# A graph attention kernel: the queries of the last node blocks made after the walk's first gathers are issued, instead of in the projection

## The chip, the cores and the metric

The kernel runs on one core of one Trainium2 chip. The metric is device microseconds of one execution. A profile is one execution that the hardware profiler recorded; its span reaches from the first to the last instruction.

## The reference

A graph layer on 12,500 nodes with 256 features and 200,000 edges that are sorted by their target `dst`. `D` is 32, there are 8 heads.

```python
h = relu(layernorm(x))
q = (h @ Wq + bq);  k = (h @ Wk + bk);  v = (h @ Wv + bv)      # heads of 32
logits = einsum('ehd,ehd->eh', q[dst], k[src]) / sqrt(32)
attn = softmax of logits over the edges with the same dst
agg = segment_sum(attn[:, :, None] * v[src], dst)
y = h + gelu(agg + h @ Wskip + bskip)
out = x + layernorm(y) * gamma + beta
```

## The kernel before

**Projection.** `project()` (from L154) goes over 98 blocks of 128 nodes, in 23 groups of 1, 2, 4, then sixteen times 5, then 4, 4, 2 and 1 blocks (`sizes`, `starts`). For each block TensorE (PE) turns `h` with the help of an identity matrix (L141), ScalarE (ACT) copies the turned `h` from PSUM to `hT` (L143), PE multiplies it with `w_kv` into `ps_kv` (L258) and with `w_q` into `ps_q` (L264). VectorE (DVE) adds the biases (L261 for k and v, L268 for q). q is stored as two parts: ACT rounds it to fp32r (L269, the high part), GpSimd (POOL) takes the difference (L270, the low part). For each group the sync engine's queue (SP) stores `h` to `h_tab`, k and v to `kv_tab` (L273) and the two parts of q to `q_pc` (L275). Wq and bq are multiplied by 1/sqrt(32) once, at the start.

**Plan.** In the same stretch `make_plan()` turns the lists of edges into tables for the walk: `idx` (which rows to gather), `e_tab`, `pen_tab`, `d0_row`, `slot_row` and a flag. Its `behind` puts some of its instructions behind given blocks of the projection, in the fixed order of an engine: a share of the list `biased` (one entry for each q addition, L268) or of `products` (one entry for each product with `w_kv` or `w_q`). A flag read by each engine then decides between `walk_streams` and another way that isn't taken here (L350).

**Walk.** `walk_streams()` goes over the edges in 66 steps. The edges are cut into 8 streams; a step takes up to 3 tiles (`j`) of 128 edges from each. For one tile, 8 indirect DMAs on POOL (`gather`, L1058) fetch the rows of k and v by `src`, 128 rows of 2 KB each. There are 6 tiles for this, 3 for each of two steps. SP loads `et` (`prefetch`, L1030), `pen` (`penalties`, L1036) and the q rows of the nodes in the step's windows, `qw` (`windows`, 8 loads at L1050 from `q_pc`). PE and ACT make a matrix `to_e` from `et` (`hot_e`, L1075 and L1077), PE spreads q over the edges with it (`spread`, L1098), DVE multiplies with k (`times`, L1107) and sums over each head (`total`, L1114). After maxima over the segments (L1133 to L1136) and the exponential (L1140), DVE weighs v (`weigh`, L1162, with L1167 or L1169 for the denominators), and PE sums per node (L1192). SP stores the sums to `table`.

Every instruction of the walk goes through `keep`, which orders it behind the one before it on the same engine; so each engine's order is the order in which the program writes the calls.

At the start of the walk the program writes: `prefetch`, `penalties` and `windows` of step 0, `prefetch` and `penalties` of step 1, then the gathers of steps 0 and 1 (48 in all, with `windows(1)` and `prefetch(2)` between them on SP), then `hot_e` of step 0, `spread`, `hot_e` of step 1, and the first multiplications. The next gathers come from `gather_next`, two at a time: the first two of them fill tile 1 of step 0 anew and stand behind `weigh(0, 1)`.

**Final pairs.** From the step `FIN_FIRST` = 10 on, pairs of blocks whose sums are complete are finished within the walk. Class `Pair` takes its tiles from the pool `fin`: `sums`, `x_f`, `h`, `o` with two buffers each, and `hT` with one. It turns `h` in a bank of `hot_ps` (transposes at L858, copy at L861), multiplies with `w_s` (L878), and so on. `hot_ps` and `qe_ps` have two PSUM buffers each. Until step 10 the tiles of `fin` lie unused.

Of the kernel before, what the change touches and what calls it, by code (L numbers as in the profile page):

```python
# [28 lines left out]
F32 = mybir.dt.float32  # L29
F32R = mybir.dt.float32r  # L30
# [4 lines left out]
OP = mybir.AluOpType  # L35
# [4 lines left out]
PSUM = bass.MemoryType.PSUM  # L40
DRAM = bass.MemoryType.DRAM

P = 128
# [28 lines left out]
def gnn_kernel(ctx: ExitStack, tc: tile.TileContext, x, src, dst, Wq, bq, Wk, bk, Wv, bv,  # L72
               Wskip, bskip, gamma, beta, out):
    nc = tc.nc
    N, HID = x.shape
    E = src.shape[0]
    D = HID // HEADS
    KC = HID // P
    SUMS = HEADS * (D + 1)
    KV = 2 * HID  # L80
    NBLK = N // P + 1
# [6 lines left out]
    h_tab = dram.tile([NP, HID], F32, name="h_tab")  # L88
# [56 lines left out]
    def norm_stats(pool, t, mean, rstd):  # L145
# [8 lines left out]
        nc.scalar.activation(rstd, mv[:, :, 1], AF.Sqrt, bias=eps)  # L154
        nc.vector.reciprocal(rstd, rstd)

    def project():


# [3 lines left out]
            tc.add_manual_dep(ins.ins, other.ins.name, mybir.DependencyInfo(  # L163
                mybir.DependencyClass.NoSync, mybir.DependencyReason.DATA), reason="kept order")

        sizes = [1] * NBLK
        if NBLK >= 14:
            mid = NBLK - 14
            sizes = [1, 2, 4] + [5] * (mid // 5) + [mid % 5] * (mid % 5 > 0) + [4, 2, 1]
        with tc.tile_pool(name="proj_c", bufs=1) as cpool, \  # L170
                tc.tile_pool(name="proj", bufs=2) as pool, \
                tc.tile_pool(name="proj_ps", bufs=2, space=PSUM) as psum:
# [11 lines left out]
                    nc.sync.dma_start(xt[:N % P, 0, :], x[b0 * P:, :])  # L184
                return xt

            starts = [sum(sizes[:i]) for i in range(len(sizes))]
            x_in = [load(0, sizes[0])]
            w_kv = cpool.tile([P, KC, 2 * HID], F32, name="w_kv")
            b_kv = cpool.tile([P, 2 * HID], F32, name="b_kv")  # L190
# [6 lines left out]
                rows(t, a)  # L197
            weights(w_q, Wq)
            rows(b_q, bq)
            qscale = 1.0 / math.sqrt(D)  # L200

            def prepare(g):

# [30 lines left out]
            for g, (b0, n) in enumerate(zip(starts, sizes)):  # L234

                if g > 1 and g + 1 < len(sizes):
                    ready[g + 1] = prepare(g + 1)
                if g == (4 if len(sizes) < 16 else 13):
                    make_near(tc, near, near_n, lambda ins: behind(ins, last))
                if g == (3 if len(sizes) < 16 else 12):  # L240
                    for ins in [rows(gam, gamma)] + \
                            [weights(w_s, Wskip)]:
                        behind(ins, products[-1])
                    pieces(b_s3, bskip, 1.0)
                    pieces(b_o3, beta, 1.0)
                    zero = cpool.tile([WN, HID], F32, name="zero")
                    nc.vector.memset(zero, 0.0)
                    for k in range(2):
                        behind(nc.scalar.dma_start(q_pc[NP:, k * HID:(k + 1) * HID], zero),
                               products[-1])  # L250
                h = ready.pop(g)
                kvo = pool.tile([P, 5, KV], F32, name="kvo")[:, :n, :]
                qp = pool.tile([P, 5, 2, HID], F32R, name="qp")[:, :n]
                for b in range(n):
                    hT, turned = transposed(pool, psum, h[:, b, :])
                    ps_kv = psum.tile([P, 2 * HID], F32, name="ps_kv", bufs=3)
                    for c in range(KC):
                        ins = nc.tensor.matmul(ps_kv, hT[:, c, :], w_kv[:, c, :], start=c == 0,  # L258
                                               stop=c == KC - 1)
                    products.append(ins)  # L260
                    nc.vector.tensor_tensor(kvo[:, b, :], ps_kv, b_kv, op=OP.add)  # L261
                    ps_q = psum.tile([P, HID], F32, name="ps_q", bufs=1)
                    for c in range(KC):
                        ins = nc.tensor.matmul(ps_q, hT[:, c, :], w_q[:, c, :], start=c == 0,  # L264
                                               stop=c == KC - 1)
                    products.append(ins)
                    q = qp[:, b, 1, :].bitcast(F32)
                    biased.append(nc.vector.tensor_tensor(q, ps_q, b_q, op=OP.add))  # L268
                    nc.scalar.copy(qp[:, b, 0, :], q)  # L269
                    nc.gpsimd.tensor_tensor(qp[:, b, 1, :], q, qp[:, b, 0, :].bitcast(F32),  # L270
                                            op=OP.subtract)
                for tab, t in ((h_tab, h), (kv_tab, kvo)):
                    nc.sync.dma_start(tab[b0 * P:(b0 + n) * P, :]  # L273
                                      .rearrange("(p b) d -> p b d", p=P), t)
                nc.sync.dma_start(q_pc[b0 * P:(b0 + n) * P, :]  # L275
                                  .rearrange("(p b) d -> p (b d)", p=P),
                                  qp.rearrange("p b k d -> p (b k d)").bitcast(F32))
                if g < 2:
                    ready[g + 1] = prepare(g + 1)
        return products, biased  # L280

    def queries(q_tab):

        with tc.tile_pool(name="qry", bufs=2) as pool:
            for b in range(NBLK):
                t = pool.tile([P, 2, HID], F32, name="q_in")
                nc.sync.dma_start(t, q_pc[b * P:(b + 1) * P, :]
                                  .rearrange("p (k d) -> p k d", k=2))
                q = pool.tile([P, HID], F32, name="q")
                nc.vector.tensor_add(q, t[:, 0, :], t[:, 1, :])  # L290
                nc.sync.dma_start(q_tab[b * P:(b + 1) * P, :], q)
# [58 lines left out]
    with tc.If(fits > 0) as branch:  # L350
        table = dram.tile([S, NT, KV], F32, name="table")
        walk_streams(tc, N, HID, NST, KL, many, ident, idx, d0_row, slot_row, near, near_n, e_tab, pen_tab,
                     h_tab, kv_tab, q_pc, table, x, out, w_s, one_row, b_s3, b_o3, gam, eps)
    with branch.Else():
        gtab = dram.tile([NP + P, SUMS + HEADS], F32, name="gtab")
        q_tab = dram.tile([NP, HID], F32, name="q_tab")
        queries(q_tab)
        walk_partitions(tc, src, dst, N, NP, HID, ident, flag, q_tab, kv_tab, gtab, dram)
        with tc.tile_pool(name="gfin", bufs=2) as pool, \
# [63 lines left out]
def make_plan(tc, pool, ep, psum, src, dst, N, LEN, NST, SLACK, NT, dram, ident, flag, idx, d0_row,  # L423
# [4 lines left out]
    nc = tc.nc  # L428
# [3 lines left out]

    def behind(ins, share):

        tc.add_manual_dep(ins.ins, biased[len(biased) * share // 100].ins.name,
                          mybir.DependencyInfo(mybir.DependencyClass.NoSync,
                                               mybir.DependencyReason.DATA), reason="kept order")

# [327 lines left out]


def walk_streams(tc, N, HID, NST, KL, many, ident, idx, d0_row, slot_row, near, near_n, e_tab, pen_tab, h_tab,
                 kv_tab, q_pc, table, x, out, w_s, one_row, b_s3, b_o3, gam, eps):

# [4 lines left out]
    nc = tc.nc  # L775
# [200 lines left out]
    with ExitStack() as es:  # L976
# [247 lines left out]
        extra = [m for m in rest if m >= SURE]  # L1224
        rest = [m for m in rest if m < SURE]

        prefetch(0)
        penalties(0)
        windows(0)
        prefetch(1)  # L1230
        penalties(1)
        for c in range(2):
            for j in range(tiles_of(c)):
                gather(c, j)
            if c == 0:
                windows(1)
                prefetch(2)
        for i in range(QT):
            hot_e(0, i)
        for half in range(2):  # L1240
# [611 lines left out]
```

## Time and profile before

| what | value |
|---|---|
| median of 3 runs | 2433.07 us (2431.04 to 2437.38) |
| profiled execution | 2429.78 us, its span 2428.1 us |
| granted TensorE clock, mean | 0.743 |

By stages of the profile, busy us of each engine, granted clock and GB/s moved:

| stage, us from the span's start | length | PE | DVE | ACT | POOL | clock | GB/s |
|---|---|---|---|---|---|---|---|
| projection and plan, up to block 81 (0 to 287.2) | 287.2 | 253.2 | 226.4 | 111.8 | 124.3 | 0.99 | 264 |
| projection, last 16 blocks, and the branch (287.2 to 338.4) | 51.2 | 44.6 | 29.6 | 12.5 | 19.6 | 1.00 | 255 |
| walk, first 48 gathers (338.4 to 398.8) | 60.4 | 25.0 | 33.4 | 12.6 | 45.8 | 0.50 | 255 |
| walk, the other gathers (398.8 to 2336.0) | 1937.2 | 1313.7 | 1663.4 | 896.1 | 1471.5 | 0.71 | 277 |
| end (2336.0 to 2428.1) | 92.1 | 60.8 | 44.1 | 28.4 | 3.3 | 0.67 | 89 |

A line of the timeline gives start, length, engine, line and operation, with the written tile to the left of the arrow and the read ones to its right; in brackets stands how long the engine had been idle and what released it. `SPq` is the sync engine's DMA queue; its lengths are those of the issue, not of the transfer. A line of the chain of waits gives start, length and what the chain ran through.

### The profile page before, as it was taken

Reading aid. Unit: us, or ns where it says so; the run is one execution under the profiler, and the core shown is the slowest. Engines: PE = TensorE matmul, PEld = TensorE weight load, DVE = VectorE, ACT = ScalarE, POOL = GpSimd, SP = SyncE. Lnnn points to the kernel's source line nnn. Section 1 sums busy time; section 2 is a strip of 40 time slices with the busy share of each in tenths; the row PEclk is TensorE's granted clock in tenths of the full one; section 3 lists DMA queues with packets and bytes.
Section 4 is the critical chain, followed back from the end, with each engine's and each line's share of the span. In section 5 each row is a group of like instructions: output and inputs, shape, how many; then the busy total and the mean of one; then the engine's idle time right before and its main releaser. Section 6 shows DMA issues by size and latency. Waiting matters only on the chain.

```text
span 2428.1 us, 29469 instructions
## 1 busy us (share of the span) xinstructions
PE 1697.2 (70%) x7824; PEld 904.4 (37%) x7824; DVE 1996.9 (82%) x2461; ACT 1061.4 (44%) x2323; POOL 1664.4 (69%) x1751
## 2 busy tenths in 40 slices
PE   6999974555556766667667777676777677667685
PEld 3555532222233333333333333333333333334343
DVE  7579946777788888888988888888888888988873
ACT  4333322333334545545545545455454455455443
POOL 4433547777777777777777777777777777777730
PEclk9999975666667777766767767677677677776666
DMA  7776678888888888988888888888888889988961
GB/s 272 293 265 260 235 257 249 255 256 255 255 269 275 285 279 286 285 274 285 286 284 280 280 291 279 276 285 285 279 281 275 285 270 285 295 269 285 291 189 56
DMA packets 305551, 649.32 MB, mean 267 GB/s; under 512 B 52836, under 2 KB 191470, under 8 KB 300378
## 3 DMA queue, kind: packets, MB, share of 16 engines
q0 software_dynamic: 129056, 424.02, 55.7%
q1 hardware_dynamic: 175570, 222.67, 27.1%
q8 instruction: 64, 1.05, 0.2%
q14 instruction: 113, 0.93, 0.1%
q10 hardware_dynamic: 748, 0.66, 0.1%
HBM read 538.91 MB, written 108.23 MB: 267 GB/s over the span
## 4 chain that ended last, share of the span: by engine, by line
DMA 27%; PE 22%; DVE 18%; issue 12%; POOL 11%; ACT 7%; SPq 3%; DVEq 0%; another core or an unknown queue 0%; POOLq 0%; ACTq 0%
DMA kv<-kv_tab,idx 18%; POOL kv L1058 10%; PE ps_kv L258 5%; DVE kv L1107 4%; DVE vw L1162 4%; PE ps_a L878 4%; DVE L L1114 4%; PE ps_q L264 3%; DMA h<-h_tab 3%; PE ps_qe L1098 2%; DMA out_dram<-o 2%; PE ps_a L1192 1%; DMA sums<-table 1%; PE ps_hot L920 1%; SPq L845 1%
## 5 line engine op out<-in xcount | busy, mean ns | idle before, releaser
L1058 POOL DMA_INDIRECT kv<-kv_tab,idx x1576 | 1517.3, 963 | 482.6 <-issue 339.2
L1107 DVE TENSOR_TENSOR kv<-ps_qe,kv 128x1024 f32<-128x1024 f32 x394 | 470.7, 1219 | 213.8 <-DMA kv<-kv_tab,idx 140.3
L1114 DVE TENSOR_REDUCE L<-kv 128x64 f32<-128x2048 f32 x197 | 450.4, 2286 | 6.9 <-DVE kv L1107 0.2
L1162 DVE TENSOR_TENSOR vw<-ps_x,kv 128x2048 f32<-128x2048 f32 x197 | 449.4, 2281 | 3.6 <-PE ps_x L1149 2.7
L1098 PE MATMUL ps_qe<-qw,to_e 64*128 64x256 f32 (+1 forms) x1576 | 310.2, 392 | 108.9 <-DVE kv L1107 105.8
L1077 ACT ACTIVATE to_e<-ps_hot,ones 128x384 fp32r<-128x384 f32 x396 | 210.5, 573 | 316.3 <-PE ps_hot L1075 307.8
L1098 PEld LDWEIGHTS ps_qe<-qw,to_e 64*128 64x128 f32 (+1 forms) x1576 | 221.8, 246 | 274.4 <-DVE kv L1107 168.5
L1192 PE MATMUL ps_a<-vw,to_n 128*32 128x264 f32 (+1 forms) x2344 | 276.5, 504 | 0.0
L1122 PE MATMUL ps_x<-ident,L 128*64 128x128 f32 x197 | 72.7, 369 | 281.4 <-DVE vw L1169 210.7
L1206 ACT COPY sums_w<-ps_a 128x264 f32<-128x264 f32 x129 | 48.8, 379 | 482.1 <-PE ps_a L1192 426.7
L1075 PE MATMUL ps_hot<-et,near 48*128 48x384 bf16 x396 | 142.5, 420 | 126.8 <-ACT to_e L1077 122.3
L258 PE MATMUL ps_kv<-w_kv,hT 128*128 128x512 f32 x392 | 192.4, 612 | 16.0 <-ACT hT L143 15.0
L270 POOL TENSOR_TENSOR qp<-qp 128x256 fp32r<-128x256 f32 x98 | 96.3, 983 | 154.7 <-ACT qp L269 154.4
L878 PE MATMUL ps_a<-w_s,hT 128*128 128x256 f32 x352 | 164.6, 648 | 19.5 <-ACT hT L861 16.7
L1192 PEld LDWEIGHTS ps_a<-vw,to_n 128*32 128x32 f32 (+1 forms) x2344 | 99.6, 139 | 197.1 <-issue 161.4
L1122 PEld LDWEIGHTS ps_x<-ident,L 128*64 128x64 f32 x197 | 24.7, 126 | 374.6 <-DVE vw L1169 300.6
L1212 ACT COPY kv<-ps_a 1x264 f32<-1x264 f32 x388 | 143.0, 369 | 6.4
L1192 PE MATMUL ps_hot<-vw,to_n 128*64 128x264 f32 x808 | 139.4, 494 | 0.0
L878 PEld LDWEIGHTS ps_a<-w_s,hT 128*128 128x128 f32 x352 | 110.5, 329 | 65.7 <-ACT hT L861 41.8
L1010 ACT ACT_TABLE_LOAD x101 | 129.6, 1283 | 1.7
L1088 ACT ACTIVATE to_n<-ps_hot,ones 128x384 f32<-128x384 f32 x197 | 103.7, 578 | 53.4 <-PE ps_hot L1086 51.2
L264 PE MATMUL ps_q<-w_q,hT 128*128 128x256 f32 x392 | 103.1, 386 | 8.3 <-DVE qp L268 8.2
(288 smaller groups left out, 2111.8 us busy)
## 6 DMA issues: line engine op xcount, KB each, us to landing
qw<-q_pc SPq DMA_DIRECT2D x264, 128.0 KB
kv<-kv_tab,idx POOLq DMA_INDIRECT x1576
kv_tab<-kvo SPq DMA_DIRECT2D x16, 1280.0 KB
q_pc<-qp SPq DMA_DIRECT2D x16, 1280.0 KB
qw<-q_pc SPq DMA_DIRECT2D x264, 64.0 KB
table<-sums_w SPq DMA_DIRECT2D x260, 61.9 KB
pen<-pen_tab SPq DMA_DIRECT2D x66, 192.5 KB
sums<-table SPq DMA_DIRECT2D x90, 132.0 KB
```

The lines of the kernel that those rows point to most:

```text
L258: ins = nc.tensor.matmul(ps_kv, hT[:, c, :], w_kv[:, c, :], start=c == 0, stop=c == KC - 1)
L264: ins = nc.tensor.matmul(ps_q, hT[:, c, :], w_q[:, c, :], start=c == 0, stop=c == KC - 1)
L878: self.keep(nc.tensor.matmul(self.ps[:, b, :], self.hT[:, b, c, :], w_s[:, c, :], start=False, stop=False, skip_group_check=True))
L1058: ins = keep(nc.gpsimd.indirect_dma_start(out=t[:, s, :], out_offset=None, in_=kv_tab[:, :], in_offset=bass.IndirectOffsetOnAxis(ap=idx[:, ...
L1075: keep(nc.tensor.matmul(ps[:, :CH], near[:, i * P:(i + 1) * P], step[c]["et"], start=True, stop=True))
L1077: keep(nc.scalar.activation(step[c]["to_e"][:, i, :], ps[:, :CH], AF.Relu, scale=-1.0, bias=ones))
L1098: keep(nc.tensor.matmul(ps[:, b, a, :], g["to_e"][at:at + w, i, j * P:(j + 1) * P], g["qw"][at:at + w, i, :], start=True, stop=True))
L1107: keep(nc.vector.tensor_tensor(k, g["qe", half].rearrange("p b a d -> p a b d"), k, op=OP.mult))
L1114: keep(nc.vector.tensor_reduce(g["L"][:, j, :].rearrange("p (s h) -> p s h", s=S), g["kv"][j][:, :, :HID].rearrange("p s (h d) -> p s h d" ...
L1162: keep(nc.vector.tensor_tensor(t[:, :, HEADS:].rearrange("p s (h d) -> p s h d", h=HEADS), wj[:, :, :, None].to_broadcast([P, S, HEADS, D] ...
L1192: keep(nc.tensor.matmul(ps[at:at + w, :], g["to_n"][:, j, i * P + at:i * P + at + w], g["vw"][j][:, s, :], start=j == turns(c)[0], stop=j ...
L1212: keep(nc.scalar.copy(step[c + 1]["kv"][0][0:1, s, HID - HEADS:], ps[at:at + 1, :]))
```

## The change

The blocks from `LATE` on get no q in the projection: their groups make and store only k, v and `h`. `LATE` is the first group's start that is at least `NBLK - 24` and leaves an even number of blocks. A new function `late_queries` makes their q from the stored `h`, two blocks at a time. In the walk it stands behind the issue of the 48 gathers and uses the tiles of `fin` and the banks of `hot_ps` and `qe_ps`. It loads Wq and bq into the two buffers of `sums` and scales them; the `prefetch` and `penalties` of steps 0 and 1 are issued within it, behind its first loads; `windows` of steps 0 and 1 and `prefetch(2)` come after it. The plan's `behind` now counts shares of the number of blocks instead of the length of `biased`. The way that isn't taken calls the same function with tiles of its own. The low part of a late q is taken on DVE instead of POOL.

```diff
+    LATE = next((b for b in starts if b >= NBLK - 24 and (NBLK - b) % 2 == 0), NBLK)
+    def late_queries(tile, transposed_ps, product_ps, keep, meanwhile=lambda: None):
+        w_q = tile("sums", KC * HID).rearrange("p (c n) -> p c n", c=KC)
+        b_q = tile("sums", HID)
+        keep(nc.sync.dma_start(w_q, Wq.rearrange("(c p) n -> p c n", p=P)))
+        keep(nc.sync.dma_start(b_q, bass.AP(tensor=bq.tensor, offset=bq.offset,
+                                            ap=[[0, P], [1, HID]])))
+        pairs = range(LATE, NBLK, 2)
+        def fetched(b0):
+            h = tile("h", 2 * HID).rearrange("p (b d) -> p b d", b=2)
+            keep(nc.sync.dma_start(h, h_tab[b0 * P:(b0 + 2) * P, :]
+                                   .rearrange("(p b) d -> p b d", p=P)))
+            return h
+        def transposes(h):
+            ps = transposed_ps()
+            for b in range(2):
+                for c in range(KC):
+                    keep(nc.tensor.transpose(ps[:, b, c, :], h[:, b, c * P:(c + 1) * P], ident))
+            return ps
+        ahead = [fetched(b0) for b0 in pairs[:2]]
+        meanwhile()
+        for t in (w_q, b_q):
+            keep(nc.vector.tensor_scalar(t, t, qscale, None, op0=OP.mult))
+        turned = [transposes(ahead.pop(0))] if ahead else []
+        for i, b0 in enumerate(pairs):
+            hT = tile("hT", 2 * KC * P).rearrange("p (b c d) -> p b c d", b=2, c=KC)
+            keep(nc.scalar.copy(hT, turned.pop()))
+            if i + 1 < len(pairs):
+                turned.append(transposes(ahead.pop(0)))
+            ps = product_ps()
+            for b in range(2):
+                for c in range(KC):
+                    keep(nc.tensor.matmul(ps[:, b, :], hT[:, b, c, :], w_q[:, c, :],
+                                          start=c == 0, stop=c == KC - 1))
+            hi = tile("x_f", 2 * HID).rearrange("p (b d) -> p b d", b=2)
+            lo = tile("o", 2 * HID).rearrange("p (b d) -> p b d", b=2)
+            keep(nc.vector.tensor_tensor(lo, ps, b_q[:, None, :].to_broadcast([P, 2, HID]),
+                                         op=OP.add))
+            keep(nc.scalar.copy(hi.bitcast(F32R), lo))
+            keep(nc.vector.tensor_tensor(lo.bitcast(F32R), lo, hi, op=OP.subtract))
+            if i + 2 < len(pairs):
+                ahead.append(fetched(pairs[i + 2]))
+            for k, t in enumerate((hi, lo)):
+                keep(nc.sync.dma_start(q_pc[b0 * P:(b0 + 2) * P, k * HID:(k + 1) * HID]
+                                       .rearrange("(p b) d -> p b d", p=P), t))
...
                     nc.vector.tensor_tensor(kvo[:, b, :], ps_kv, b_kv, op=OP.add)
+                    if b0 >= LATE:
+                        continue
                     ps_q = psum.tile([P, HID], F32, name="ps_q", bufs=1)
...
-        tc.add_manual_dep(ins.ins, biased[len(biased) * share // 100].ins.name,
+        tc.add_manual_dep(ins.ins, biased[min(len(biased) - 1, (N // P + 1) * share // 100)].ins.name,
...
-        prefetch(0)
-        penalties(0)
-        windows(0)
-        prefetch(1)
-        penalties(1)
         for c in range(2):
             for j in range(tiles_of(c)):
                 gather(c, j)
-            if c == 0:
-                windows(1)
-                prefetch(2)
+
+        def of_fin(name, n):
+            shape = {"sums": [P, 2, SUMS], "hT": [P, 2, KC, P]}.get(name, [P, 2, HID])
+            t = fin.tile(shape, F32, name=name, bufs=1 if name == "hT" else 2)
+            return t.rearrange("p a b c -> p (a b c)" if name == "hT" else
+                               "p a b -> p (a b)")[:, :n]
+
+        def first_loads():
+            for c in range(2):
+                prefetch(c)
+                penalties(c)
+
+        late_queries(of_fin, lambda: hot_ps.tile([P, 2, KC, P], F32, name="ps_hot"),
+                     lambda: qe_ps.tile([P, 2, 2, HID], F32, name="ps_qe")[:, 0], keep, first_loads)
+        windows(0)
+        windows(1)
+        prefetch(2)
         for i in range(QT):
             hot_e(0, i)
```

More of the change, by code (lines that the diff above doesn't have):

```diff
@@ L155, in norm_stats @@
         nc.vector.reciprocal(rstd, rstd)
+    sizes = [1] * NBLK
+    if NBLK >= 14:
+        mid = NBLK - 14
+        sizes = [1, 2, 4] + [5] * (mid // 5) + [mid % 5] * (mid % 5 > 0) + [4, 2, 1]
+    starts = [sum(sizes[:i]) for i in range(len(sizes))]
+    LATE = next((b for b in starts if b >= NBLK - 24 and (NBLK - b) % 2 == 0), NBLK)
+    qscale = 1.0 / math.sqrt(D)
+    def late_queries(tile, transposed_ps, product_ps, keep, meanwhile=lambda: None):
[42 more added lines that the diff above has]
+                                       .rearrange("(p b) d -> p b d", p=P), t))
@@ L164, in behind @@
                 mybir.DependencyClass.NoSync, mybir.DependencyReason.DATA), reason="kept order")
[L166 to L169, printed above, removed]
         with tc.tile_pool(name="proj_c", bufs=1) as cpool, \
@@ L185, in load @@
                 return xt
-            starts = [sum(sizes[:i]) for i in range(len(sizes))]
             x_in = [load(0, sizes[0])]
@@ L199, in project @@
             rows(b_q, bq)
-            qscale = 1.0 / math.sqrt(D)
             def prepare(g):
@@ L252, in project @@
                 kvo = pool.tile([P, 5, KV], F32, name="kvo")[:, :n, :]
-                qp = pool.tile([P, 5, 2, HID], F32R, name="qp")[:, :n]
+                if b0 < LATE:
+                    qp = pool.tile([P, 5, 2, HID], F32R, name="qp")[:, :n]
                 for b in range(n):
@@ L274, in project @@
                                       .rearrange("(p b) d -> p b d", p=P), t)
-                nc.sync.dma_start(q_pc[b0 * P:(b0 + n) * P, :]
-                                  .rearrange("(p b) d -> p (b d)", p=P),
-                                  qp.rearrange("p b k d -> p (b k d)").bitcast(F32))
+                if b0 < LATE:
+                    nc.sync.dma_start(q_pc[b0 * P:(b0 + n) * P, :]
+                                      .rearrange("(p b) d -> p (b d)", p=P),
+                                      qp.rearrange("p b k d -> p (b k d)").bitcast(F32))
                 if g < 2:
@@ L352, in gnn_kernel @@
         walk_streams(tc, N, HID, NST, KL, many, ident, idx, d0_row, slot_row, near, near_n, e_tab, pen_tab,
-                     h_tab, kv_tab, q_pc, table, x, out, w_s, one_row, b_s3, b_o3, gam, eps)
+                     h_tab, kv_tab, q_pc, late_queries, table, x, out, w_s, one_row, b_s3, b_o3, gam, eps)
     with branch.Else():
@@ L356, in gnn_kernel @@
         q_tab = dram.tile([NP, HID], F32, name="q_tab")
+        with tc.tile_pool(name="lq", bufs=2) as pool, \
+                tc.tile_pool(name="lq_ps", bufs=2, space=PSUM) as psum:
+            late_queries(lambda name, n: pool.tile([P, n], F32, name="l_" + name),
+                         lambda: psum.tile([P, 2, KC, P], F32, name="ps_lt"),
+                         lambda: psum.tile([P, 2, HID], F32, name="ps_lq"), lambda ins: ins)
         queries(q_tab)
@@ L768, in walk_streams @@
 def walk_streams(tc, N, HID, NST, KL, many, ident, idx, d0_row, slot_row, near, near_n, e_tab, pen_tab, h_tab,
-                 kv_tab, q_pc, table, x, out, w_s, one_row, b_s3, b_o3, gam, eps):
+                 kv_tab, q_pc, late_queries, table, x, out, w_s, one_row, b_s3, b_o3, gam, eps):
     nc = tc.nc
```

## The prediction

> **What bounds the kernel now.** I read the table of stages first, then the gathers alone in slices of 60 us, then the chain of waits around the seam between projection and walk, then that seam in order of time. The gathers (L1058) on POOL, in slices over the walk; the columns are the slice, its length, busy us and count, granted clock, DMA share, GB/s:
>
> ```profile
> 338.00:398.00 60.00, 45.31 (x48) 0.50 0.83 254
> 398.00:458.00 60.00, 45.36 (x49) 0.61 0.83 254
> 1298.00:1358.00 60.00, 45.67 (x48) 0.72 0.90 288
> 2258.00:2318.00 60.00, 45.66 (x48) 0.70 0.89 284
> ```
>
> Every slice holds 47 to 49 gathers, from first to last: one per 1.26 us (0.95 busy and 0.30 before the next). From the 49th gather (398.82) to 2336 there are 1528 of them in 1937 us, 1.268 each, so only some 15 us in all are waits. POOL issues without a pause and sets the walk's length: what moves the 49th gather moves the end by as much, unless POOL catches up, which it can't at a fixed 1.26 us. DVE is 86% busy over that stretch and always a little behind the gathers.
>
> The chain of waits in the last blocks of the projection (start, us, what):
>
> ```profile
> 316.27 1.98 PE ps_kv L258 x4
> 318.25 0.86 PE ps_q L264 x4
> 319.12 1.72 PE ps_kv L258 x4
> 320.83 0.86 PE ps_q L264 x4
> 322.01 0.38 ACT hT L143
> ...
> 335.81 1.79 DMA q_pc<-qp
> ```
>
> Here PE is the bound, two blocks in 6.16 us, 2 x 0.86 of it q; then the last q store must land (337.60) before POOL gathers. The seam itself, in order of time:
>
> ```profile
> 333.92 0.33 SPq L273 DMA_DIRECT2D kv_tab<-kvo  x1
> 338.36 1.04 POOL L1058 DMA_INDIRECT kv<-kv_tab,idx  x1 [2.58 <-DMA et<-e_tab]
> 338.60 4.53 SPq L1050 DMA_DIRECT2D qw<-q_pc  x8
> 347.85 1.23 DVE L1107 TENSOR_TENSOR kv<-ps_qe,kv 128x1024 f32<-128x1024 f32 x1 [11.44 <-DMA kv<-kv_tab,idx]
> 386.76 0.22 DVE L1169 COPY vw<-ps_x 128x64 f32<-128x64 f32 x1
> 398.82 0.95 POOL L1058 DMA_INDIRECT kv<-kv_tab,idx  x1 [0.30 <-issue]
> ```
>
> Six tiles hold 48 gathers. The 49th reuses tile 1 of step 0 and may go only when DVE has weighed it (L1162 and L1169, done at 386.98). Before, that was 11.8 us early: this is all the slack that the walk's start has. DVE's own work in that time (window, us, busy us and count, clock, share, GB/s):
>
> ```profile
> 347.85:386.98 39.13, 25.32 (x19) 0.50 0.86 266
> ```
>
> 25.3 us of work in 39.1: the rest was gathers that hadn't landed.
>
> **The change, part by part.**
>
> *Which blocks.* `LATE` is the first group start at or past block 74 that leaves an even rest. The starts run 72, 77, 82, 87; 77 leaves 21. So 82: 16 blocks in 8 pairs move, not 24. The order of instructions agrees: 82 q products stay, 8 pairs stand behind the branch.
>
> *Removed from the projection.* 16 x 0.86 = 13.8 us of PE, on the path. The last store to wait for becomes kv's, issued 1.9 us before q's (333.92 against 335.81): together 15.7. The first gather comes at 338.36 - 15.7 = 322.7. Covers: DVE is busy 29.6 of the last 51.2 us and loses 16 x 0.41; ACT 12.5. If the plan's long DVE work or the stores held PE up after all, I'd expect 10 instead of 15.7; more than 16.5 is excluded, since nothing else goes. The plan's kept order on PE and DVE stays put: its indices come out at the same blocks.
>
> *Added behind the gathers' issue.* The gathers stand first on POOL and need nothing of the new work. On SP, though, the loads of qw (L1050) for steps 0 and 1 come after all of it, and DVE's first multiplication needs them. New on SP: Wq, bq, 8 h loads, 16 q stores; on PE 32 transposes and 32 products; on ACT 16 copies; on DVE 2 scalings and 16 additions or subtractions. `keep` holds them in order, and hT has one buffer. Prices, from the walk's pairs, which do the same shapes (timeline; chain of waits):
>
> ```profile
> 785.67 0.56 ACT L861 COPY hT<-ps_hot 128x512 f32<-128x512 f32 x1
> 786.29 3.78 PE L878 MATMUL ps_a<-w_s,hT 128*128 128x256 f32 x8 [0.23 <-ACT hT L861]
> ```
>
> ```profile
> 810.17 6.24 DMA h<-h_tab
> ...
> 901.92 5.38 DMA h<-h_tab
> ...
> 921.41 4.49 DMA h<-h_tab
> ```
>
> A pair's products take 3.78 at clock 0.5 and 1.95 at full clock (the projection's 0.86 x 2, and its start). Four transposes take 1.3 (L858, 0.63 + 0.69) or 0.65. DVE adds or subtracts 128x512 in 0.68 (L261, L890); ACT's copy to hi has no row of its shape: 0.41 for half of it (L269) and 0.56 (L861) bound it, I take 0.57. An h load lands after 4.5 to 6.2 us under gathers, I take the middle, 5.4. Which clock? Two slices of PE alone at the seam:
>
> ```profile
> 336.00:338.00 2.00, 0.00 (x0) 1.00 0.43 149
> 338.00:340.00 2.00, 1.00 (x3) 0.55 0.31 100
> ```
>
> After 4.5 us without a matmul the clock falls to half and is 0.50 as far as 398. The new work starts after such a gap too. In the walk it took from 786 to 795 with PE at 80% to 100% busy until it rose again. The new pairs load PE by 5.1 us of 6.6, with gaps, so I take 0.5.
>
> The Trainium skill (TensorE: Matmul & The Clock Gate, Part 1: The HAM clock gate) says that the clock is halved by default and freed after some 3.4 us of sustained work. The first half agrees with these rows; the second would make most pairs run at full clock, a pair in 5.4 us, and by it my sum would be about 8 us lower. The row of 786 to 795 is slower than the rule, and I go by it.
>
> *One pair.* Between products of neighbouring pairs on ACT and DVE: add 0.68, hi 0.57, copy of hT 0.57, handovers 0.4: 2.2, with 3.78 a period of 6.0. The other loop is longer: the load of h for pair i+2 stands on SP behind the stores of pair i-1. From the end of products i-1: add, hi, subtract with handovers 2.25; issue of the lo store 0.35; landing 5.4; transposes 1.3, handovers 0.2; products i+1 3.78: 13.3 us per two pairs, 6.64 each.
>
> *The sum,* from Wq's issue (the landing of the last kv store, 0.7 before the first gather: 322.0). Four issues and the first landing: transposes begin at 5.5 (4.6 to 6.5), two sets of them to 8.1, first products end at 11.9. Pairs 2, 4 and 6 later: + 3 x 13.3 = 51.8. The last pair's h is long there: + 6.0 = 57.8. Add, hi, subtract, issue: 60.4. Store lands after 4 (1.8 as q_pc above, unloaded, to 6.2): 64.4. Four qw loads issued (4 x 0.57) and landed (2, the gathers having ended; before it was some 5): 68.7; first products: 69.6. So the first multiplication stands at 391.6 instead of 347.85. All gathers have landed by then, and DVE runs on its 25.3 us plus gaps for qw's second half, the step's `to_e` and the scan: 28 (26 to 30). The weighing ends at 97.6, and the 49th gather goes at 322.0 + 97.9 = 419.9, against 398.82: + 21.1 us. POOL, done with 48 by 383, stands idle some 36 us.
>
> *Later.* After the 49th gather DVE needs some 25 us for a step and POOL 30.2, and a gather's release is never later than POOL's turn, by 2 to 5 us at the tightest; so POOL saturates again at once and the shift reaches the end undiminished. `et` and `pen` of steps 0 and 1 now wait behind Wq and two h loads; they are needed long after.
>
> The profiled execution (2429.8, its span 2428.1) would become 2450.9; the three runs have their median 3.3 above it, 2433.1, so I predict 2454.
>
> **Rivals.**
>
> A. *The work is faster than I sum.* Full clock and loads in 4.5: the loop is 9.9 per two pairs; first products end at 7.9, the last at 7.9 + 29.7 + 4.2 = 41.8, qw used at 51.2, weighing done at 78.2: + 2 us, about 2435. For it: PE is fairly busy. Against: the clock row, and a DMA share of 0.83 that now gets 6.7 MB more.
>
> B. *The DMA queues are the bound.* 48 gathers bring 12.6 MB (128 rows of 2 KB each), the new work 6.7 MB (24 transfers of 0.26, and 0.39 for Wq and bq); in 60 us that is 322 GB/s, over every 60 us slice (294 at most). Loads at 7.5 us, stores at 6, and a gain of only 10 in the projection give + 37: 2470. For it: the slices' share of 0.83 to 0.93.
>
> C. *Faster: the work is truly hidden.* Place: the wait of the 49th gather. If the weighing is done within 60.4 us of the first gather, the 15.7 us stay whole: 2417. It decides at a first multiplication 33 us after Wq's issue (any gain at all: 48 us), that is pairs of 2 to 3.7 us. For it: half of the engines' time there is idle. Against: one pair alone, with products, add, hi and copy in series, takes 4.1 even at full clock and with loads at nothing.
>
> **How the numbers follow.** A measurement of this kernel tells about 0.3% (7 us) from no change. My sum 0.70, A 0.14, B 0.10, C 0.06. Of A 0.08 lies within 0.3% and 0.06 above it. Slower by over 0.3%: 0.70 + 0.10 + 0.06 = 0.86; within: 0.08; faster: 0.06. The range runs from A's end, 2435, to B's, 2470; C is left out.
>
> **What would show it.** First gather near 323; first L1107 (in new lines) near 392; loads of h 4.5 to 6.2 us apart from their transposes; granted clock 0.5 up to 385; 49th gather near 420 behind a gap of some 36 us that ends with a DVE weighing; after it 48 gathers per 60 us again. I am wrong if that gap is missing, or if POOL catches up later.

## The result and the profile after

| | before | after |
|---|---|---|
| median | 2432.06 us (2426.9 to 2437.38, 6 runs) | 2457.56 us (2450.81 to 2467.92, 6 runs) |
| profiled execution, its span | 2429.78, 2428.1 us | 2458.51, 2456.9 us |
| first gather | 338.36 us | 324.48 us |
| first multiplication (L1107, now L1168) | 347.85 us | 393.61 us |
| 49th gather | 398.82 us | 420.97 us |
| span less 49th gather | 2029.3 us | 2035.9 us |

The ratio after to before is 1.0097, with an interval of 1.008 to 1.0113: slower by 25.5 us, where 21 were predicted. The gathers stand at L1119 in the changed kernel. In slices of 60 us (slice, length, POOL's busy us on them and their count, granted clock, DMA share, GB/s):

```profile
323.00:383.00 60.00, 44.51 (x47) 0.69 0.91 297
383.00:443.00 60.00, 18.75 (x20) 0.60 0.53 164
443.00:503.00 60.00, 45.37 (x49) 0.63 0.85 259
2303.00:2363.00 60.00, 45.51 (x48) 0.74 0.88 277
```

Before, every slice held 47 to 49. Now the second holds 20, and all later ones are full again: one gap, and nothing is caught up. Some 22 of the 25.5 us stand at the 49th gather; the rest is within the scatter of the walk's length that the runs below show. Some lines of the seam, in order of time, show what is in the gap:

```profile
324.48 1.05 POOL L1119 DMA_INDIRECT kv<-kv_tab,idx  x1 [18.79 <-issue]
388.76 9.69 SPq L1111 DMA_DIRECT2D qw<-q_pc  x16
393.61 1.22 DVE L1168 TENSOR_TENSOR kv<-ps_qe,kv 128x1024 f32<-128x1024 f32 x1 [9.42 <-PE ps_qe L1159]
420.62 0.21 DVE L1230 COPY vw<-ps_x 128x64 f32<-128x64 f32 x1
420.97 0.95 POOL L1119 DMA_INDIRECT kv<-kv_tab,idx  x1 [35.77 <-DVE vw L1230]
```

The 48 gathers start 13.9 us earlier, as wished. But `qw` is loaded only at 388.76, so the first multiplication is 45.8 us later than before, and the 49th gather waits 35.77 us for DVE's weighing, which frees its tile. The chain of waits through the late pairs (start, us, what) says why `qw` is so late:

```profile
324.89 6.10 DMA h<-h_tab
331.00 1.94 PE ps_hot L185 x8
332.94 3.74 PE ps_qe L201 x8
336.70 0.70 DVE o L205
337.43 0.63 ACT x_f L207
338.08 0.70 DVE o L208
338.80 0.56 SPq L212
339.36 0.05 issue
339.46 5.99 DMA h<-h_tab
...
384.22 4.53 DMA q_pc<-o
388.76 0.59 SPq L1111
```

An h load stands on SP behind the stores of the pair three before it (338.80 ahead of 339.46), and the products of the pair before it wait for its transposes. So products, sums, stores and a load follow each other in a ring of two pairs, which is run through three times in all; then the last store must land, and only then may `qw` be read.

### The profile page after: what moved, and what is told of

Its sections match the earlier page's. It is cut to its first block, busy times and chain, and to the rows that moved or that the text cites. A ratio compares the mean times of both kernels' runs of the same rounds, so it can differ in the third digit from the quotient of the medians.

```text
span 2456.9 us, 29588 instructions
## 1 busy us (share of the span) xinstructions
PE 1720.0 (70%) x7856; PEld 914.8 (37%) x7856; DVE 2003.3 (82%) x2463; ACT 1064.5 (43%) x2323; POOL 1649.9 (67%) x1735
## 4 chain that ended last, share of the span: by engine, by line
DMA 27%; PE 20%; DVE 20%; issue 12%; POOL 10%; ACT 6%; SPq 2%; DVEq 0%; ACTq 0%; POOLq 0%
DMA kv<-kv_tab,idx 18%; POOL kv L1119 10%; DVE kv L1168 5%; PE ps_kv L311 5%; DVE vw L1223 4%; DMA h<-h_tab 4%; DVE L L1175 4%; PE ps_a L939 3%; PE ps_qe L1159 2%; PE ps_q L319 2%; PE ps_a L1253 2%; ACT L1071 1%; DMA sums<-table 1%; DMA out_dram<-o 1%; SPq L906 1%
## 5 line engine op out<-in xcount | busy, mean ns | idle before, releaser
L1119 POOL DMA_INDIRECT kv<-kv_tab,idx x1576 | 1522.7, 966 | 534.4 <-issue 369.4
L1168 DVE TENSOR_TENSOR kv<-ps_qe,kv 128x1024 f32<-128x1024 f32 x394 | 471.6, 1218 | 195.9 <-DMA kv<-kv_tab,idx 114.7
L939 PE MATMUL ps_a<-w_s,hT 128*128 128x256 f32 x352 | 164.1, 646 | 20.7 <-ACT hT L922 17.8
L325 POOL TENSOR_TENSOR qp<-qp 128x256 fp32r<-128x256 f32 x82 | 76.2, 929 | 130.5 <-ACT qp L324 130.3
L311 PEld LDWEIGHTS ps_kv<-w_kv,hT 128*128 128x128 f32 x392 | 71.1, 192 | 79.5 <-issue 48.7
```

Source lines behind the costliest of these rows:

```text
L939: self.keep(nc.tensor.matmul(self.ps[:, b, :], self.hT[:, b, c, :], w_s[:, c, :], start=False, stop=False, skip_group_check=True))
L1119: ins = keep(nc.gpsimd.indirect_dma_start(out=t[:, s, :], out_offset=None, in_=kv_tab[:, :], in_offset=bass.IndirectOffsetOnAxis(ap=idx[:, ...
L1168: keep(nc.vector.tensor_tensor(k, g["qe", half].rearrange("p b a d -> p a b d"), k, op=OP.mult))
```

## Experiments

All with the chip's own runs of the kernel before beside them. Four runs fell on another chip, on which before takes 2986.38 us; they are told last. What the profiled executions show on the chips with before at 2431.86 to 2433.5:

| kernel | first gather | first multiplication | 49th gather | span less 49th | median us | ratio to before |
|---|---|---|---|---|---|---|
| without late pairs, extra zero stores | 370.40 | 380.5 | 430.86 | 2032.1 | 2465.78 | 1.0133 (1.0095 to 1.0171) |
| q of all blocks, and the late pairs | 338.66 | 405.7 | 433.45 | 2031.2 | 2468.63 | 1.0151 (1.0122 to 1.018) |
| h one pair further ahead | 325.82 | 384.5 | 412.93 | 2032.1 | 2448.28 | 1.0059 (1.0038 to 1.0081) |
| both windows ahead | 324.75 | 396.4 | 422.78 | 2042.2 | 2460.79 | 1.0107 (1.0078 to 1.0135) |
| without late pairs, k and v stored for q | 329.10 | 338.6 | 389.59 | 2033.5 | 2425.66 | 0.9968 (0.9955 to 0.9981) |
| h ahead and `windows(0)` ahead | 324.05 | 376.7 | 402.87 | 2028.6 | 2441.11 | 1.0025 (1.001 to 1.0039) |
| one pair in each of steps 0 to 7 | 323.40 | 333.7 | 383.88 | 2038.4 | 2424.58 | 0.9961 (0.9946 to 0.9976) |
| 11 pairs in steps 0 to 10 | 338.87 | 349.1 | 399.47 | 2037.5 | 2438.51 | 1.0015 (1.0 to 1.003) |

The four columns after the name are of the profiled execution, the last two of all runs. With both windows ahead the profiled execution was the longest of 4 (2466.76), with h and `windows(0)` ahead the shortest of 10 (2433.2).

**The late pairs left out, first try.** In place of `late_queries`, and in the projection behind the stores of the zero rows:

```diff
+                        behind(nc.scalar.dma_start(
+                            q_pc[LATE * P:NP, k * HID:(k + 1) * HID]
+                            .rearrange("(p r) d -> p r d", p=WN),
+                            zero[:, None, :].to_broadcast([WN, (NP - LATE * P) // WN, HID])),
+                            products[-1])
...
-        late_queries(of_fin, lambda: hot_ps.tile([P, 2, KC, P], F32, name="ps_hot"),
-                     lambda: qe_ps.tile([P, 2, 2, HID], F32, name="ps_qe")[:, 0], keep, first_loads)
+        first_loads()
```

> The late pairs are left out: the q of the last 16 blocks are not made, zeros are stored in their place during the projection, so the output is wrong for their nodes; all else is the changed kernel. Theory (the 49th gather waits for DVE, which waits for qw, which waits for the late pairs; before it the projection gained 14 us): first gather near 324, the first multiplication some 10 us behind it, no gap on POOL, 49th gather at 324 + 60.4 = 384.5, time 2432 - 14 = 2418 (2412 to 2424). Rival (the loss lies in the rest of the walk, by a lower clock or more traffic, or the projection gained nothing that reaches the end): 2430 or more.

Slower instead, for a reason of its own. The projection's PE in slices (slice, length, busy us and count of PE, weight loads, DVE, ACT and POOL, clock, DMA share, GB/s):

```profile
200.00:220.00 20.00, 7.48 (x12) 3.58 (x12) 6.42 (x14) 1.64 (x5) 2.41 (x4) 0.67 0.98 264
220.00:240.00 20.00, 4.90 (x16) 3.51 (x17) 9.63 (x33) 2.65 (x7) 1.45 (x2) 0.54 0.30 78
```

PE works 7.5 and 4.9 of 20 us, where it works 19.5 and 19.8 in after: the added 4.2 MB of zeros fill the DMA engines (0.98), and DVE, whose bias additions PE needs, waits 21.45 us for a load of the plan. The first gather comes at 370, 46 us later than in after. These two slices hold 27 of that; where the rest arose isn't settled. The time says nothing of the theory. The shape agrees with it: no gap at the 49th gather, and a first multiplication 10 us after the first gather.

**The late pairs left out, clean.** The 16 blocks' q rows get k and v, by the store that wrote q before; `first_loads()` stands in place of `late_queries` as in the first try:

```diff
-                if b0 < LATE:
-                    nc.sync.dma_start(q_pc[b0 * P:(b0 + n) * P, :]
+                nc.sync.dma_start(q_pc[b0 * P:(b0 + n) * P, :]
...
-                                      qp.rearrange("p b k d -> p (b k d)").bitcast(F32))
+                                  qp.rearrange("p b k d -> p (b k d)").bitcast(F32)
+                                  if b0 < LATE else kvo.rearrange("p b d -> p (b d)"))
```

> The kernel of the second try without late pairs again, because its first measurement fell on a chip on which the kernel of before takes 2986 us (its walk is slower by a quarter there, its projection is not). The late pairs are left out and the q rows of the last 16 blocks filled with k and v, by stores of the same bytes. On a chip with before at about 2432 the theory gives: first gather 324 to 328, first multiplication 10 us later, no gap of POOL ahead of the 49th gather, at about 386; 2417 to 2424, ratio 0.994 to 0.997. Rival (the 14 us are lost elsewhere): 2432 or more. On a chip like the last: 0.996 again.

2425.66, just above the span expected. The first gather was later than thought, 329.10 and not 324 to 328, and the edit itself is the reason: the stores to `q_pc` now read the tile `kvo`, and the next bias additions into that tile wait for them.

```profile
325.20 0.69 DVE L314 TENSOR_TENSOR kvo<-ps_kv,b_kv 128x512 f32<-128x512 f32 x1 [3.61 <-DMA q_pc<-kvo]
```

In after this last addition stands at 320.55, 4.6 us earlier, which is the whole difference at the first gather. (The DMA share over 280 to 325 is 0.89, against 0.69 in after.) From there it is as expected: the 49th gather, at 389.59, goes without a gap, 60.5 us after the first, where it takes 96.5 in after. So the seam costs 36 us, of which 31.4 remain between the two 49th gathers and 31.9 between the two times (2457.56 - 2425.66). The seam's price is that of the late pairs ahead of the first step's work, and nothing else that the change does costs time that these runs can tell. By which engine the pairs hold that work up, this run doesn't tell.

**The work doubled: q also kept in the projection.**

```diff
-                if b0 < LATE:
+                if True:
                     qp = pool.tile([P, 5, 2, HID], F32R, name="qp")[:, :n]
...
-                    if b0 >= LATE:
-                        continue
...
-                if b0 < LATE:
+                if True:
                     nc.sync.dma_start(q_pc[b0 * P:(b0 + n) * P, :]
```

> The projection makes the q of all 98 blocks as before, and the late pairs make those of the last 16 once more. Theory: the seam's cost stands alone, without the gain: first gather at 338 to 339, first multiplication 69 later, 49th gather at 338.4 + 96.5 = 435, time 2432 + 36 = 2468 (2462 to 2474). Rival (the gain in the projection is not passed on to the first gather, or the loss is made by the short tail of the projection): no more than the changed kernel, 2457.

As expected: 2468.63 and 433.45. With no gain ahead of it, the same seam moves the 49th gather by 34.6 us. The two parts of the change add: 34.6 less the 13.9 of the projection is 20.7, near the 22.15 by which after's 49th gather is later.

**The h load one pair further ahead**: that of pair i + 3 is issued right behind the transposes of pair i + 1, ahead of the stores of pair i instead of behind them:

```diff
+        if len(pairs) > 2:
+            ahead.append(fetched(pairs[2]))
...
+            if i + 3 < len(pairs):
+                ahead.append(fetched(pairs[i + 3]))
...
-            if i + 2 < len(pairs):
-                ahead.append(fetched(pairs[i + 2]))
```

> The h load of pair i+3 is issued on SP when the transposes of pair i+1 are, ahead of the q stores of pair i, instead of behind those of the pair before. Theory (the longer loop of a pair is the h load behind the stores): two pairs take 2 x (3.6 + 2.2) = 11.6 us instead of 14.3, three times, so the 49th gather comes 8 us earlier (16 if PE then keeps the full clock), time 2449 (2441 to 2451). Rival (the DMA queues are saturated and set the pace, not the order on SP): the loads land as late as before, 2457.

2448.28, with the 49th gather 8.04 us earlier than in after, as expected. The loads themselves landed no sooner (6.31 and 7.33 us in its chain of waits), so it is the ring through SP that the pairs waited for.

**Both windows ahead of the late pairs** on SP:

```diff
+        windows(0)
+        windows(1)
         late_queries(of_fin, lambda: hot_ps.tile([P, 2, KC, P], F32, name="ps_hot"),
                      lambda: qe_ps.tile([P, 2, 2, HID], F32, name="ps_qe")[:, 0], keep, first_loads)
-        windows(0)
-        windows(1)
```

> The qw loads of steps 0 and 1 stand on SP ahead of the late pairs; on PE, ACT and DVE all stays as in the changed kernel. Steps 0 and 1 touch no node of the late blocks. Theory: of the late stage only the part behind the last subtraction goes: the landing of the last store (4.5 us) and most of the first qw loads (4.8 us), while hot_e and the spread still stand behind the products on PE: first multiplication near 388 instead of 393.6, 49th gather 6 to 8 us earlier, time 2450 (2447 to 2453). Rival (SP's order alone holds the walk, the engines' order does not): first multiplication soon after the first gathers land, time 2418 to 2425.

A miss: 2460.79, the 49th gather 1.8 us later than in after. SP's queue in order of time:

```profile
323.95 10.04 SPq L1111 DMA_DIRECT2D qw<-q_pc  x16
334.50 0.39 SPq L170 DMA_DIRECT2D sums<-in_L_gnn_Wq_dram  x1
```

The 16 issues take 10 us at either place. At the end the chain of after has only the first 4 of them, 2.6 us (388.76 to 391.36), with a landing of 2.24 and the last store's of 4.53: 9.4 us that the move saves. At the front they delay Wq, and with it the whole ring, by 11.0 us (334.50 against 323.48). My expectation had priced the wait that goes and not the queue that the loads were moved past. The rival fell too: `qw` was issued by 334.0, yet the first multiplication comes at 396.44. On PE the first step's `to_e` and spread stand behind the last late products (389.05), and the spread starts at 395.85. So SP's order isn't all that holds the walk.

**h ahead and `windows(0)` alone ahead**, the eight issues put behind those of Wq, of the first h loads and of `et` and `pen`:

```diff
         def first_loads():
             for c in range(2):
                 prefetch(c)
                 penalties(c)
+            windows(0)
...
-        windows(0)
         windows(1)
```

> h loads one pair further ahead and windows(0) ahead of the late work, again, for the same reason. With before at about 2432: 49th gather 6 us earlier than with the h loads alone (412.9), at about 407, and 2443, if the two waits add; 2448 if the second gain is lost, because the SP issues of qw take 0.6 to 1 us each among the first gathers and the third h load stands behind them.

The gains add, and a little more: the 49th gather goes at 402.87, 10.1 us ahead of the run with h ahead alone. The median, 2441.11, is 7.2 below that run's. PE's own order of time, without the later transposes:

```profile
344.59 1.09 PE L185 MATMUL ps_hot<-ident,h 128*128 128x128 f32 x4 [8.46 <-DMA h<-h_tab]
345.47 3.62 PE L205 MATMUL ps_qe<-sums,hT 128*128 128x256 f32 x8
351.00 1.99 PE L205 MATMUL ps_qe<-sums,hT 128*128 128x256 f32 x8 [1.18 <-ACT hT L197]
354.92 1.99 PE L205 MATMUL ps_qe<-sums,hT 128*128 128x256 f32 x8 [1.48 <-ACT hT L197]
358.83 1.99 PE L205 MATMUL ps_qe<-sums,hT 128*128 128x256 f32 x8 [0.88 <-ACT hT L197]
...
370.71 1.99 PE L205 MATMUL ps_qe<-sums,hT 128*128 128x256 f32 x8 [2.04 <-ACT hT L197]
372.64 0.50 PE L1138 MATMUL ps_hot<-et,near 48*128 48x384 bf16 x2
...
376.09 1.56 PE L1161 MATMUL ps_qe<-qw,to_e 64*128 64x256 f32 x8
```

After one long wait for h (8.46, behind `qw`'s issues) the pairs run one per 3.92 us, a little under the 4.1 that the prediction gave as the least for one pair. The first multiplication, at 376.71, no longer waits for `qw` (issued by 336.2) but for PE, where `to_e` (372.64) and the spread (376.09) follow the last late products. So the late pairs hold the walk at two places: on SP ahead of `qw`, and on PE ahead of the first step's own products. Even so the 49th gather is 4 us later than before the change, after POOL has stood idle for 17.18 us, and the kernel isn't faster than before (1.0025).

**One pair in each of the steps 0 to 7.** `et`, `pen` and `qw` are issued as before the change; Wq and bq come behind them, and `late_queries` becomes a generator whose five parts run between a step's own calls: the h load where a final pair fetches its own; transposes, copy and products into a bank of `ag_ps` where such a pair has its skip product; and, further on, the addition, the high part, and the low part with both stores. The first three places:

```diff
             if pair:
                 pair.fetch()
+            late_part()
             maxima(c)
...
                 pair.skip()
+            late_part()
...
             gather_next(c, 0, 3)
+            late_part()
```

This serves lists of edges whose first windows need no late row. Here stream 7 starts at node 9559 and reaches block 82 (node 10496) near step 21; for other lists the plan's flag would have to test it.

> One late pair in each of the steps 0 to 7, again, for the same reason. With before at about 2432: first gather 324 to 326, first multiplication 10 us later, no gap at the 49th gather, at about 386. Theory (the seam is what costs): 2418 to 2430. Rival, sharpened by the first measurement (14 us more than without late pairs): the pairs' 6.3 MB of loads and stores now move in steps whose DMA engines are at 0.89, and at 281 GB/s take 22 us: 2432 to 2440, no gain over before.

2424.58, within the theory's span, and faster than before: 0.9961 (0.9946 to 0.9976). POOL goes from the 48th to the 49th gather without a pause (383.88). The rival (the pairs' transfers crowd the steps) holds in part at most. The window that holds six of the eight pairs:

```profile
425.00:800.00 375.00, 241.80 (x1216) 125.09 (x1212) 306.80 (x269) 142.09 (x330) 284.76 (x297) 0.67 0.88 276
```

The same window in before:

```profile
425.00:800.00 375.00, 217.32 (x1131) 108.12 (x1130) 296.79 (x248) 130.93 (x305) 284.24 (x298) 0.65 0.84 261
```

POOL issues 297 gathers there, as in before (298): the added work of PE, DVE and the DMA engines is in the row, and the pace of the gathers is the same to one gather, 1.3 us. Of the 14.9 us at the 49th gather, 8.8 arrive at the median. Against the run without late pairs the 49th gather is 5.7 us earlier and the median 1.1 lower, which leaves up to 4.6 us, 0.6 a pair, for the steps. But the walk's length scatters by more among these kernels (2028.6 to 2042.2), so whether the steps cost something stays open.

**11 pairs in the steps**, with one of the projection's two groups of 4 blocks behind the fives moved ahead of them, so that a group starts at block 76:

```diff
-        sizes = [1, 2, 4] + [5] * (mid // 5) + [mid % 5] * (mid % 5 > 0) + [4, 2, 1]
+        sizes = [1, 2, 4] + [mid % 5] * (mid % 5 > 0) + [5] * (mid // 5) + [4, 2, 1]
```

> The late pairs in the walk's steps again, and more of them: the projection's groups in the order 1, 2, 4, 4, then fives, 4, 2, 1, so that a group starts at block 76 and 22 blocks (11 pairs, in steps 0 to 10) move instead of 16. Theory: the projection is shorter by 6 x 0.86 = 5.2 us more, first gather at about 318.5, no gap at the 49th gather, at about 379; the three added pairs cost in their steps what the other eight do (the run with eight came out 1 us below the run without late pairs, with its first gather 5.7 us earlier: 0.6 us a pair), so 2424.6 - 5.2 + 1.8 = 2421, ratio 0.995. Rival (the steps have no room for the pairs' transfers, or the first gather is set by the queue of stores and not by PE): 2424 to 2430, no better than with eight pairs. On a chip on which before takes 2986: the same differences hold for the first gather and the 49th, the time is not told apart.

A miss ahead of the walk: the first gather comes at 338.87, not 318.5, and the median, 2438.51, lies above both spans. One of the causes is in the order of time of PE and DVE:

```profile
291.94 0.60 PE L141 MATMUL ps_t<-ident,h 128*128 128x128 f32 x4
296.46 0.43 DVE L306 BATCH_NORM_STATS2 st<-x_in 128x6 f32<-128x256 f32 x1 [9.78 <-DMA x_in<-in_x_dram]
300.90 6.57 PE L353 MATMUL ps_kv<-w_kv,hT 128*128 128x512 f32 x8 [8.36 <-DVE kvo L356]
```

DVE stands 9.78 us for a load of x; PE stands 8.36 us for the bias addition that comes behind this on DVE, and starts at half clock afterwards (6.57 for products that take 3.70 elsewhere). That is 11 of the 20 us. Some 5 more lie between 190 and 250 us, where PE is busy for 53.2 us against 58.2 in after. Why that load was late, and what made the rest, stays open. In the walk itself the three added pairs show no cost in this one execution: span less 49th gather 2037.5, against 2038.4, with the scatter named above.

**The other chip.** The first measurement of four kernels fell on it.

> The late pairs are left out: no Wq reload, no h loads, no products at the seam. The q rows of the last 16 blocks are filled with k and v by the same store, of the same bytes, that before used for q; so the attention of their edges is computed from other numbers, while the projection's stores and everything in the walk keep their size. Unlike the first try without late pairs, nothing is added to the projection's queues. Theory (the late pairs delay the 49th gather, nothing else of the change costs time): first gather 324 to 326 us, first multiplication 10 us after it, no gap of POOL ahead of the 49th gather, which comes 61 us after the first (48 x 1.26) at about 386; with span minus 49th gather of 2029 to 2036 (before and after) the time is 2417 to 2424. Rival (the 1.05 us or so per step that the walk of after takes beyond before is a property of the changed walk, or the 14 us from the projection are lost in another queue): first gather at 335 or later, or 2432 and more.

> windows(0), 8 issues of qw on SP, moves ahead of the late queries' work but behind the issue of Wq, bq, the first two h loads and et and pen; windows(1) and et(2) stay behind. Theory (the first multiplication of after waits for the 16 qw issues of 0.6 us behind the last q store, and only the first 8 are needed for it): Wq is issued at 323.5 as in after, the 8 issues take 5 us that end before the third h load can be issued, first multiplication 6 us earlier than in after at about 388 and 49th gather at about 415; 2451. Rival (what gave back the gain in the run with both windows ahead was not the issue of Wq but the 8 MB/s share of the qw transfers among the gathers, or the multiplication waits for something else): first multiplication 393 or later and 2458.

> h loads one pair further ahead and windows(0) ahead of the late work, together. Theory (two separate waits on one chain, so the gains add): 49th gather 8 us earlier from the one and 6 from the other, at about 407; time about 2443. Rival (the loop is then bound by the transfers of h and q among the gathers, with the DMA engines at 0.94, so that the second gain is lost): as with the h loads alone, 2448.

> The same late pairs, none of them at the seam: one pair in each of the walk's steps 0 to 7, its h load, transposes, products, sums and stores put between the step's own work; et, pen and qw are issued as in before. The first windows of nodes of this list of edges need no late rows. Theory (the seam is what costs, the work itself is small: 8 pairs of 1.4 us on DVE and 5 us on PE): first gather at 324 to 325, first multiplication 10 us later, no gap of POOL ahead of the 49th gather, at about 386; time 2418, plus at most the 11 us of DVE if DVE has no room in these steps, so 2418 to 2430 and faster than before. Rival (the pairs' PE and DVE work stands on the chain of each step, which DVE and POOL leave no room in): 8 steps longer by 5 us each, 2440 to 2460.

(Two figures in these texts are in no run: the 16 loads of `qw` hold 1.6 MB, 4 of 128 KB and 4 of 64 KB in each step, and the walk of after is 6.6 us longer than that of before in 66 steps, 0.1 per step.)

Against before at 2986.38: without late pairs 2977.4, ratio 0.996 (0.9938 to 0.9983); `windows(0)` ahead 3019.56, 1.0098 (1.0063 to 1.0134); both 3011.03, 1.0097 (1.0066 to 1.0127); in the steps 2991.82, 1.0015 (1.0 to 1.003). The kernel without late pairs in the same window, first there and then on the usual chip:

```profile
1000.00:1500.00 500.00, 301.60 (x1303) 157.70 (x1303) 333.86 (x345) 190.59 (x401) 291.77 (x304) 0.65 0.71 217
```

```profile
1000.00:1500.00 500.00, 356.39 (x1749) 186.58 (x1747) 438.97 (x460) 247.29 (x522) 380.00 (x394) 0.72 0.89 281
```

304 gathers instead of 394 in 500 us, and no engine is fuller; POOL isn't what sets the walk there. The same transfers land later (the gap ahead of the 49th gather is 17.35 us even with no late pairs), eight issues of `qw` took up to 17.60 us on SP against 4.5 to 8, and the h loads further ahead, added to `windows(0)` ahead, moved the 49th gather by only 1.1 us (447.77 to 446.67). The changed kernel itself was not measured there. `windows(0)` ahead was measured alone only there, so its own share on the usual chip is read from the pair of runs above.

## Why the prediction was right, step by step

*POOL sets the walk, and the 49th gather carries over to the end.* Right, on the chips with before near 2432. Over ten executions whose 49th gather lies between 383.88 and 433.45, the span less that gather stays between 2028.6 and 2042.2. On the other chip POOL isn't full.

*First gather at 322.7.* It came at 324.48, a gain of 13.9 instead of 15.7, within the bounds given. PE's last product ends 13.5 us earlier (320.5 against 334.0), where 13.8 were worked out. The 1.9 for the store was the mis-sized term: 0.9 came of it, since kv's store goes 0.75 us after the last product and lands in 1.96; and 0.5 was lost between landing and gather. That the plan's kept order stays at the same blocks was right for `biased` and wrong for `products`: that list fell from 196 to 180 entries, so the transposes that hang on it moved from blocks 49 to 63 to blocks 45 to 58. They still ran at 193.8 to 237.4 us, against 193.3 to 236.5.

*First transposes 5.5 us after Wq's issue.* 7.5 (331.00 against 323.48), outside the bounds of 4.6 to 6.5. Here the sum itself was off: 5.5 for four issues and a landing priced at 5.4 leaves 0.1 for the issues, and those ahead of the load took 1.4 (324.89 less 323.48). The landing took 6.10. All loads in the chain were slow: 6.10, 5.99, 5.48, 6.24 against 5.4. The rows that gave 5.4 are of loads of 128 KB, the late pairs' loads are of 256 KB; and they share the DMA engines with the gathers, at a share of 0.94 and 309 GB/s from 325 to 385. Which of the two made them longer, no run here tells; the second would be rival B's crowding, in a small measure.

*13.3 us per two pairs.* 13.6, 14.4 and 13.7 between the products at 332.88, 346.46, 360.90 and 374.56: the loads again, and a store's issue of 2.10 once. The run with h ahead shows that this ring is the bound.

*The clock at half throughout.* Wrong, but on the path it mattered mainly in the last pair. Four windows of PE alone (slice, length, busy us and count, clock, DMA share, GB/s):

```profile
331.00:337.00 6.00, 5.66 (x16) 0.50 1.05 324
338.00:341.00 3.00, 2.26 (x12) 1.00 0.93 306
345.00:351.00 6.00, 4.71 (x13) 0.50 1.02 380
366.00:369.00 3.00, 1.99 (x8) 1.00 0.87 249
```

The pair behind a long wait for h runs at half clock, its follower mostly at full. The first of each two was in the ring, and that one I had right. The Trainium skill (TensorE: Matmul & The Clock Gate, Part 1: The HAM clock gate) has some 3.4 us of work for the change up and one idle window of as much for the change down. These rows lie near it (full clock after 4 to 7 us of work, half after waits of 4.5 to 5.2, full kept over 2.1), and the row of 786 to 795, by which I had gone, was the exception. The prediction's estimate from the first part of that rule, 8 us lower, was further off: it took most pairs at full clock, while waits of 4.5 us and more for h kept every second pair at half.

*Last pair + 6.0, store's landing 4, `qw` used at 69.6.* The last pair, at full clock, took 3.9 from the end of the products before it, the landing 4.53. The first multiplication came 70.1 us after Wq's issue. That this is so near 69.6 is luck: the late start and the slow loads cost 3 us more than the sum had, the last pair's full clock and the quicker spread 2.5 less. *Weighing 28 us later:* 27.2. *49th gather at 419.9:* 420.97.

*The rivals.* A fell: full clock came, but, except in the last pair, only where nothing waited for it. B fell: the projection's gain was 13.9 and not 10, the loads took up to 6.24 and not 7.5, and the 49th gather moved by 22 and not 37. C's point of decision held: it asked for a first multiplication within 48 us of Wq's issue for any gain. With both waits mended it comes after 53.7 (376.7 less 323.05), and there is none. In the steps the pairs are off that path altogether, and the 49th gather goes without a gap, as C had it, though C's 2417 isn't reached (2424.58).

## What to carry to other kernels

Work put "behind" the issue of a long run of transfers is hidden only if nothing that these transfers' buffers wait for stands behind the work: here 48 gathers flew, but the loads that let DVE free the first buffer came after all the late pairs on SP, and the products that use them came after all the late products on PE. The slack to compare with is that of the first reuse, 11.8 us, not the flight time of 60. Where the same work is spread, one small piece into each step of a loop whose other engines have room, it cost some 0.6 us a piece, or nothing that these runs can tell; and a load moved ahead of others on one queue delays these by its issues, 0.6 to 1.0 us each here.

## What the runs showed of the hardware that I had not expected

- The granted clock changed from one pair to the next: in after, eight products took 3.62 to 3.78 us behind a wait of 4.5 us or more, and mostly 1.89 to 1.99 behind one of up to 2.1. Shorter waits don't settle it: 3.04 behind one of 2.41 and 1.99 behind one of 2.48 in the run with h ahead, 3.42 behind one of 1.92 in the run with both windows ahead.
- Two chips differ by 23% on the same kernel (2432 and 2986 us). The projection takes about the same on both (first gather at 329.10 and 328.47 without late pairs), while in the walk the gathers come at 304 against 394 in 500 us. What differs there wasn't settled.
- With stores of 4.2 MB, issued by ACT on top of the projection's own, its PE worked 12.4 us of 40 (7.48 and 4.90), where it works 39.2 in after.
